# Exponentials kept in one fixed SBUF tile and summed by tensor_reduce, with row sums a stretch later and more work on GpSimd

## The chip, the core and the metric

The kernel runs on one core of one Trainium2 chip. The core has TensorE (matrix products into PSUM), VectorE, ScalarE, GpSimd, and SyncE (SP), which here issues nearly all DMAs. The metric is the device time of one execution in microseconds (us). Before the change it is 2807.87 us, the median of 3 runs (2807.44 to 2809.33).

## What is computed

Two attention blocks over images of 512 channels and 32 x 32 places; 8 images, all float32. Cut to what matters:

```python
def L0(x):                                  # 8 heads of 64 channels
    h = group_norm(x, groups=32)
    q, k, v = split(einsum('oc,bct->bot', w_qkv, h) + b_qkv)
    weight = softmax(einsum('bct,bcs->bts', q * scale, k * scale), axis=-1)
    a = einsum('bts,bcs->bct', weight, v)
    return x + einsum('oc,bct->bot', w_proj, a) + b_proj

def L1(x):                                  # one head of 512 channels
    xn = group_norm(x, groups=8)
    q, k, v = conv1x1(xn, q_w, q_b), conv1x1(xn, k_w, k_b), conv1x1(xn, v_w, v_b)
    attn = softmax(einsum('bqc,bck->bqk', q, k) / sqrt(512), axis=-1)
    return x + conv1x1(einsum('bqk,bkc->bqc', attn, v), p_w, p_b)

x = L1(L0(x))
```

A softmax is computed without subtracting the maximum: exponentials, their product with the values, and a division by the sums of the exponentials afterwards.

## The kernel before

**Products.** Large products use a seven-product (Winograd) form of the 2 x 2 block product; convolutions of layer 0 use it twice, one inside the other. Each needs sums and differences of its operands ("factors"): `left_sums`, `right_sums`, `image_factors` (t, and differences in place), `inner_factors` (four differences of 128 x 256 for each of the seven products, made in the order 1, 5, 2, 6, 7, 3, 4), `query_factors`. TensorE's instructions are all pinned to the order in which the program writes them; others are pinned only where the text says `keep_in_program_order`, and otherwise ordered by a scheduler by readiness and program order.

**Layer 0's attention** (`attention0`, one call per image) goes over 4 pairs of heads (hp) and 2 halves of the queries (tb): 8 *stretches*. In a stretch, 8 times (s): two products give scores into a PSUM tile `sc` [128, 2, 512] (three such tiles, six banks), and ScalarE takes the exponential into a tile `e` of 128 x 1024 (L658). VectorE adds the eight tiles up, one add after another, into `total` (L660, L662). Then the products of values and exponentials go into `av`. ScalarE copies `av` to `a` (L681). After the second half of a head pair `scale` (L694) calls `reciprocals`: products with a column of ones add the totals over the partitions ("row sums"), VectorE copies the result to a line (L617), and a chain of DMAs on SP turns it into columns, takes it back after VectorE's reciprocal, and spreads it over the partitions as `r`. One stretch of products later VectorE multiplies `a` by `r` (L696), and SP stores it to `kept`. For the last head pair GpSimd multiplies, and the row sums come behind the first product of the next stage. In the last image (`store` is None) the output is not kept, and the order differs.

**Hooks.** Other work is put into the 8 stretches by a list `extra` of 16 hooks: number 2n is run after the scores of stretch n, number 2n + 1 after its values. In images 1 to 6 they carry the residual adds (0), group-norm statistics (1, 3), the group mean (4), its scale (5), the normalisation on ScalarE (7, 9), and the factors of the next products (9 to 15); in image 0 the factors of a weight product z (`later`), whose DMA `prepare_z<-product_z` is issued shortly before, and the first weight loads.

**Layer 1's scores** (`scores1`) go into eight tiles `e`; ScalarE takes the exponentials in place (L739), GpSimd adds them up (L743), and VectorE (four) and GpSimd (four) take the differences that the next product needs (L786). `values1` multiplies with the values; `layer1_rest` puts these together.

**Memory.** A pool `big` has 34 buffers of 4 KB per partition, shared by images, factors, exponentials and totals, each freed after its last use. PSUM has eight banks: in layer 0's attention six hold scores, and a pool `ps_acc` of two (L185) holds, in turn, `av`, row sums, and the small products for the group mean and variance (`acc_tile`, L193).

Of the kernel before, what the change touches and what calls it, by code (L numbers as in the profile page):

```python
# [15 lines left out]
P = 128  # L16
EPS = 1e-5
ORDER = (1, 5, 2, 6, 7, 3, 4)
NBIG = 34
# [10 lines left out]
def two_attention_blocks_kernel(  # L30
# [143 lines left out]
    def main_path(ctx):  # L174
        big = ctx.enter_context(tc.tile_pool(name="big", bufs=NBIG))
        wpool = ctx.enter_context(tc.tile_pool(name="wpool", bufs=3))
# [117 lines left out]
        def keep(n, t):  # L294
            nc.sync.dma_start(wdram[n], t)
# [54 lines left out]
        def image_factors(h, uid, sub=nc.vector.tensor_sub):  # L350

            tiles = [pair_tile(f"t{i}_{uid}") for i in (1, 2, 4)]
# [57 lines left out]
        def inner_factors(hf, uid, pin=lambda ins: ins, engine=nc.gpsimd):  # L410

            f, steps = {}, []
            for p in ORDER:
                t = big_tile(f"inner{p}_{uid}", (P, 4, 2 * P))
# [178 lines left out]
        def reciprocals(totals, uid, across, direct=None):  # L593
# [17 lines left out]
            queue = direct or nc.sync  # L611
            lines = lambda d: d.rearrange("t j i n -> i (t j) n"), line[0:P:32].rearrange("p t a b -> p (t a) b")
            if direct:
                nc.vector.reciprocal(line, sums)
                queue.dma_start(lines[0](rows), lines[1])
            else:
                nc.vector.tensor_copy(line, sums)  # L617
                raw_rows = rowpool.tile([n, 2, 4, P], F32, tag=f"rows{n}", name=f"rows_{uid}")
                queue.dma_start(lines[0](raw_rows), lines[1])
                cols = small.tile([P, 16], F32, tag="cols", name=f"cols_{uid}")[:, : n * 8]  # L620
                flat = lambda t: t.rearrange("t j i n -> (t j i n)").rearrange("(p m) -> p m", p=P)
                queue.dma_start(cols, flat(raw_rows))
                recs = small.tile([P, 16], F32, tag="recs", name=f"recs_{uid}")[:, : n * 8]
                nc.vector.reciprocal(recs, cols)
                queue.dma_start(flat(rows), recs)
            if across:
                r = pair_tile(f"r_{uid}")
                for j in range(2):
                    row = rows[0, j : j + 1].rearrange("j i n -> j (i n)")
                    queue.dma_start(r[:, j, :], row.to_broadcast([P, HT]))  # L630
            else:
                r = rpool.tile([P, 2, HT], F32, tag="r", bufs=1, name=f"r_{uid}")[:, :n]
                for j in range(2):
                    row = rows[:, j : j + 1].rearrange("t o i n -> o t (i n)")
                    queue.dma_start(r[ts(j, 64)], row.to_broadcast([64, n, HT]))
            return r


        def attention0(b, q, k, v, a, extra, store=None):
            n = 0  # L640
            scaled, totals, behind = [], [], []

            for hp in range(KC):
                for tb in (0, 1) if hp < KC - 1 or store else (1, 0):
                    uid = f"0_{b}_{hp}_{tb}"
                    total = pair_tile(f"sum_{uid}")
                    es = []
                    for s in range(NS):
# [8 lines left out]
                        e = pair_tile(f"e_{uid}_{s}")  # L657
                        nc.scalar.activation(e, sc, AF.Exp, scale=(C // 8) ** -0.5)  # L658
                        if s == 1:
                            nc.vector.tensor_add(total, es[0], e)  # L660
                        elif s > 1:
                            nc.vector.tensor_add(total, total, e)  # L662
                        es.append(e)
# [10 lines left out]
                    if not (store and hp == KC - 1):  # L674
                        after, scaled = [*scaled, *after], []
                    elif tb == 1:
                        after, scaled = [*after, *scaled], []
# [23 lines left out]
                    if store and hp == KC - 1:  # L701
                        behind.append(scale)
                    else:
                        scale()

            assert not extra
# [3 lines left out]
        def scores1(f, gf, gsteps, first, uid, stats):  # L710
# [6 lines left out]
            e = {(c, cc, r): pair_tile(f"e_{uid}_{c}{cc}{r}") for r in range(2) for c in range(2) for cc in range(2)}  # L717
            total = pair_tile(f"sum_{uid}")
            parts = [pair_tile(f"sum{r}_{uid}") for r in range(2)]
# [17 lines left out]
            def exps(r, c):  # L737
# [3 lines left out]
            def add_up(r, c):  # L741

                on = lambda dst, x, y: lambda: tc.keep_in_program_order(nc.gpsimd.tensor_tensor(dst, x, y, ALU.add))  # L743
                if r == c:
                    return [on(parts[r], e[c, 0, r], e[c, 1, r])]
                return [
                    *(on(parts[r], parts[r], e[c, cc, r]) for cc in range(2)),
                    on(total[:, r, :], parts[r][:, 0, :], parts[r][:, 1, :]),
                ]

            def product(s, p, y, x, before, small, after7=(), final=()):
# [19 lines left out]
            product(1, 2, (0, 0), (1, 0), [5], gsteps[2:4], (), [lambda: exps(0, 0)])  # L771
# [3 lines left out]
            product(5, 3, (0, 1), (0, 1), [], stats[7:10] + add_up(0, 0), [lambda: exps(1, 1)], [lambda: exps(0, 1)])  # L775
            product(
                6, 4, (1, 0), (1, 0), [], stats[10:] + add_up(1, 1) + add_up(0, 1), (),
                [lambda: exps(1, 0), lambda: background.extend(add_up(1, 0) + steps)],
# [3 lines left out]
            engines = [nc.vector] * 4 + [nc.gpsimd] * 4  # L782
# [3 lines left out]
                lambda *a: engines.pop(0).tensor_tensor(*a, ALU.subtract),  # L786
# [24 lines left out]
        def raw(n, i):  # L811
            ts_ = [pair_tile(f"raw{n}_{h}") for h in range(2)]
# [15 lines left out]
        def natural(wt, nm, banks):  # L828
            ts_ = [pair_tile(f"nat{nm}_{h}") for h in range(2)]
# [41 lines left out]
        def prologue():  # L871
            ident.append(big_tile("ident", (P, P)))
            make_identity(nc, ident[0])
            raw_k = raw("k", 5)
            raw_q = raw("q", 4)
            h0 = [load_x(0, c, "h0") for c in range(KC)]
            first = {n: prepare(n) for n in "vqk"}
            wk = natural(raw_k, "k", ("a", "b"))
            wq = natural(raw_q, "q", ("c", "acc"))
# [13 lines left out]
            raw_v = raw("v", 6)  # L893
            raw_p = raw("p", 7)
# [21 lines left out]
            wv = natural(raw_v, "v", "bc")  # L916
            norm1.group_mean(acc_tile("gmean_0_1")[:, :KC])
            for f in p0_steps:
# [9 lines left out]
                1: steps, 2: [lambda: keep("z", t), load, load], 5: [load],  # L928
                12: [
# [177 lines left out]
        for b in range(B):  # L1107
# [16 lines left out]
            hf, t = image_factors(h, uid, here)  # L1124
            inner, ih = inner_factors(hf, uid, tc.keep_in_program_order)
            V = nc.vector
# [30 lines left out]
            for f in ih[4:]:  # L1157
                f()
# [21 lines left out]
            def factors_of_a():  # L1180
                af, t = image_factors(again, f"a_{b}")
                f, ia = inner_factors(af, f"a_{b}", tc.keep_in_program_order)
# [220 lines left out]
```

## Time and profile before

| | |
|---|---|
| median of 3 runs | 2807.87 us |
| the profiled execution | 2808.09 us |
| its span (first to last instruction) | 2806.3 us |
| TensorE clock granted, mean | 0.998 |
| one layer-0 stretch on TensorE | 7.07 (scores) + 7.02 (values) us |
| one image in the steady part (900.74 to 1242.63) | 341.89 us: TensorE busy 341.75, VectorE 245.83, ScalarE 124.28, GpSimd 161.92 |
| bytes moved by DMA | 320.10 MB, 114 GB/s in the mean |

Times in a profile line are microseconds; in a group of instructions the columns are line, engine, operation, output<-inputs with their shapes, count, then busy time in us and the mean of one in ns, and last the idle time of the engine just before them with what ended it. A wait is written as "engine, tile <- releaser: us in total, times, longest". In the chain that ended last, each step is followed back to what released it; its columns are start, length, and what ran. L60 is the helper that issues all matmuls, so these are told apart by tile names: `sc` scores, `av` values, `sums` row sums.

### The profile page before, as it was taken

The numbers are of one execution on the slowest core, as the hardware profiler recorded it, in microseconds if no ns is written. First come the engines' busy times: TensorE is split into PE (matmuls) and PEld (weight loads), VectorE is DVE, ScalarE is ACT, GpSimd is POOL, SyncE is SP. The second block draws the span as 40 slices with busy tenths as digits, with TensorE's granted clock in tenths as the row PEclk, the third lists the DMA queues.
The fourth block names the chain that finished last, engine by engine and source line by source line (L and its number), as shares of the span: only waits on it lengthen the run. The fifth ranks groups of instructions, "written<-read, shape, count | busy, mean of one in ns | idle before, by whom it ended". The sixth has DMA issues, their size and how long they took to land.

```text
span 2806.3 us, 35081 instructions
## 1 busy us (share of the span) xinstructions
PE 2786.6 (99%) x12756; PEld 1749.4 (62%) x12756; DVE 1981.4 (71%) x3018; ACT 986.3 (35%) x1275; POOL 1265.5 (45%) x1300
## 2 busy tenths in 40 slices
PE   9999999999999999999999999999999999999999
PEld 5436736776376853768538594485844868348584
DVE  5477777667776777766776767766678756787665
ACT  1253354214632146312463125531255212633130
POOL 2302705745067440774308652185521846137572
PEclk9999999999999999999999999999999999999999
DMA  8744512234123441134401343114521035112301
GB/s 285 226 161 139 196 32 70 111 146 178 34 67 131 152 153 39 62 139 165 148 24 62 150 174 127 32 54 161 187 102 49 37 151 207 63 55 94 120 5 73
DMA packets 118525, 320.10 MB, mean 114 GB/s; under 512 B 19591, under 2 KB 57927, under 8 KB 107722
## 3 DMA queue, kind: packets, MB, share of 16 engines
q1 hardware_dynamic: 117758, 317.36, 31.7%
q8 instruction: 103, 1.69, 0.2%
q14 instruction: 76, 0.62, 0.1%
q10 hardware_dynamic: 588, 0.42, 0.0%
HBM read 247.13 MB, written 70.62 MB: 113 GB/s over the span
## 4 chain that ended last, share of the span: by engine, by line
PE 97%; DVE 2%; issue 1%; POOL 1%; DMA 0%; ACT 0%; SPq 0%; DVEq 0%; POOLq 0%
PE sc L60 16%; PE av L60 15%; PE psb_av L60 6%; PE psb L60 5%; PE psa_av L60 4%; PE psc_av L60 4%; PE psc L60 3%; PE psa L60 3%; PE psb_z L60 3%; PE psb_g L60 3%; PE psb_k L60 3%; PE psb_q L60 3%; PE psb_v L60 3%; PE psb_p L60 2%; PE psa_z L60 2%; PE psc_z L60 2%
## 5 line engine op out<-in xcount | busy, mean ns | idle before, releaser
L658 ACT ACTIVATE e<-sc 128x1024 f32<-128x1024 f32 x512 | 476.2, 1051 | 79.7 <-PE sc L60 79.7
L662 DVE TENSOR_TENSOR sum<-sum,e 128x1024 f32<-128x1024 f32 x384 | 470.5, 1225 | 35.8 <-ACT x L138 0.5
L60 PE MATMUL sc<-q,k 64*128 64x512 f32 x2048 | 458.4, 597 | 0.0
L60 PE MATMUL av<-e,v 128*64 128x512 f32 x2048 | 453.4, 595 | 0.0
L60 PEld LDWEIGHTS sc<-q,k 64*128 64x128 f32 x2048 | 190.7, 186 | 247.3 <-ACT e L658 120.3
L60 PEld LDWEIGHTS av<-e,v 128*64 128x64 f32 x2048 | 141.4, 137 | 299.0 <-issue 289.0
L421 POOL TENSOR_TENSOR inner_h<-x 128x256 f32<-128x256 f32 x16 | 14.8, 924 | 415.8 <-DVE x L1105 415.8
L660 DVE TENSOR_TENSOR sum<-e,e 128x1024 f32<-128x1024 f32 x64 | 79.2, 1237 | 103.7 <-ACT e L658 103.7
L681 ACT COPY a<-av 128x512 f32<-128x512 f32 x64 | 37.6, 587 | 319.4 <-PE av L60 308.1
L126 POOL TENSOR_TENSOR rstd<-ve,mhalf 128x4 f32<-128x4 f32 x16 | 16.7, 1043 | 263.9 <-DVE ve L124 263.9
L60 PE MATMUL psb<-inner,inner_h 128*128 128x256 f32 x448 | 115.6, 380 | 0.0
L60 PE MATMUL psa_av<-e,z 128*128 128x512 f32 x256 | 113.3, 595 | 0.0
L421 POOL TENSOR_TENSOR inner_h<-h 128x256 f32<-128x256 f32 x30 | 24.1, 805 | 186.9 <-DVE h L1105 119.8
L743 POOL TENSOR_TENSOR sum<-sum,e 128x1024 f32<-128x1024 f32 x32 | 81.4, 2543 | 28.9 <-ACT e L739 27.7
L60 PEld LDWEIGHTS psb<-inner,inner_h 128*128 128x128 f32 x448 | 84.5, 190 | 13.6 <-POOL inner L436 1.8
L469 ACT COPY psb_v<-psa_v 128x512 f32<-128x512 f32 (+1 forms) x28 | 14.5, 517 | 218.9 <-DVE x L805 155.1
L60 PE MATMUL psb_g<-inner_h,w_m 128*128 128x256 f32 x336 | 86.5, 385 | 0.3
L729 DVE TENSOR_TENSOR e<-psc,u 128x512 f32<-128x512 f32 x56 | 38.7, 691 | 65.5 <-PE psc L60 65.3
L542 POOL TENSOR_TENSOR v<-v,v 128x256 f32<-128x256 f32 x28 | 20.1, 727 | 143.5 <-DVE u_v L537 143.4
L60 PEld LDWEIGHTS psa_av<-e,z 128*128 128x128 f32 x256 | 48.0, 190 | 57.3 <-issue 56.6
L421 POOL TENSOR_TENSOR inner_h<-t_h 128x256 f32<-128x256 f32 x62 | 73.3, 1187 | 21.3 <-PE psc_av L60 16.1
L739 ACT ACTIVATE e<-e 128x1024 f32<-128x1024 f32 x64 | 65.3, 1053 | 46.7 <-DVE e L729 25.6
(433 smaller groups left out, 6088.6 us busy)
## 6 DMA issues: line engine op xcount, KB each, us to landing
r<-all_rows SPq DMA_DIRECT2D x78, 256.0 KB
x<-in_x SPq DMA_DIRECT2D x36, 512.0 KB
h<-in_x SPq DMA_DIRECT2D x32, 512.0 KB
spill<-x SPq DMA_DIRECT2D x32, 512.0 KB
x<-spill SPq DMA_DIRECT2D x32, 512.0 KB
out<-x SPq DMA_DIRECT2D x64, 256.0 KB
kept<-a SPq DMA_DIRECT2D x28, 512.0 KB
again<-kept SPq DMA_DIRECT2D x28, 512.0 KB
```

The costliest lines, as they stand in the source:

```text
L60: tc.keep_in_program_order(nc.tensor.matmul(*args, **kw))
L126: nc.gpsimd.tensor_tensor(rstd, ve, mhalf, ALU.pow)
L421: pin(engine.tensor_tensor(dst, x, y, ALU.subtract))
L469: nc.scalar.copy(ps["b"], ps["a"])
L542: nc.gpsimd.tensor_tensor(d, x, y, ALU.add)
L658: nc.scalar.activation(e, sc, AF.Exp, scale=(C // 8) ** -0.5)
L660: nc.vector.tensor_add(total, es[0], e)
L662: nc.vector.tensor_add(total, total, e)
L681: nc.scalar.copy(dst, av)
L729: nc.vector.tensor_add(dst[0], ps, x[0])
L739: nc.scalar.activation(e[c, cc, r], e[c, cc, r], AF.Exp, scale=scale)
L743: on = lambda dst, x, y: lambda: tc.keep_in_program_order(nc.gpsimd.tensor_tensor(dst, x, y, ALU.add))
```

## The change

- The eight exponentials of a layer-0 stretch go to fixed places of one tile `exps` of nine places of 4 KB (0 to 3 and 5 to 8). In images 0 to 6 VectorE adds places 0 to 3 into place 4 by one `tensor_reduce` after the fourth exponential, and places 4 to 8 into the total by a second after the eighth. Neighbours within a reduction are one place, 4 KB, apart. The last image keeps the adds.
- The row sums of the first three head pairs come one stretch later, after the scores; their copy to a line moves to ScalarE; the scaling comes after the values of the stretch after that, on GpSimd.
- In these images the differences of `image_factors` and all of `inner_factors` move from VectorE to GpSimd.
- In layer 1 VectorE sums the exponentials by eight `tensor_reduce` of 128 columns each, and GpSimd takes all eight differences.
- `big` has 26 buffers; raw and transposed weights of the start, the attention output that is read back (`again`) and some of its factors use places of `exps`.
- In image 0 the hooks of z's factors and of the weight loads move later.

```diff
-NBIG = 34
+NBIG = 26
...
+        epool = ctx.enter_context(tc.tile_pool(name="epool", bufs=1))
+        exps = epool.tile([P, 9, 2, HT], F32, tag="exps", name="exps")
...
-                nc.vector.tensor_copy(line, sums)
+                copy(line, sums)
...
+            sums, due = [], {}
+            after_sc, whole = exps[:, 4], lambda lo, hi: exps[:, lo:hi].rearrange("p s j n -> p (j n) s")
...
+                    flat = total.rearrange("p j n -> p (j n)")
+                    stretch = n // NS
+                    es = [exps[:, s + s // 4] for s in range(NS)]
+                    for s, e in enumerate(es):
...
                         nc.scalar.activation(e, sc, AF.Exp, scale=(C // 8) ** -0.5)
-                        if s == 1:
+                        if store:
+                            if s == 3:
+                                nc.vector.tensor_reduce(after_sc.rearrange("p j n -> p (j n)"), whole(0, 4), AX.X, ALU.add)
+                            elif s == NS - 1:
+                                nc.vector.tensor_reduce(flat, whole(4, 9), AX.X, ALU.add)
+                        elif s == 1:
                             nc.vector.tensor_add(total, es[0], e)
...
-                    for f in extra.pop(0) if extra else ():
+                    for f in [*sums, *(extra.pop(0) if extra else ())]:
                         f()
+                    sums = []
                     av = acc_tile(f"av_{uid}")
...
+                    if store:
+                        after = [*after, *due.pop(stretch, ())]
...
-                    engine = nc.gpsimd if hp == KC - 1 and not direct else nc.vector
+                    engine = nc.gpsimd if store or hp == KC - 1 and not direct else nc.vector
...
-                        r = reciprocals(totals, uid, False, nc.scalar if direct else None)
+                        copy = nc.scalar.copy if store and hp < KC - 1 else nc.vector.tensor_copy
+                        r = reciprocals(totals, uid, False, nc.scalar if direct else None, copy)
...
+                    elif hp < KC - 1:
+                        sums.append(scale)
+                        due[stretch + 2] = scaled
...
-            e = {(c, cc, r): pair_tile(f"e_{uid}_{c}{cc}{r}") for r in range(2) for c in range(2) for cc in range(2)}
+            e = {(c, cc, r): exps[:, 5 * r + 2 * c + cc] for r in range(2) for c in range(2) for cc in range(2)}
...
+            def add_up(r):
+
+                every = exps[:, 5 * r : 5 * r + 4].rearrange("p s i n -> p n (s i)")
                 return [
+                    lambda n=n: tc.keep_in_program_order(
+                        nc.vector.tensor_reduce(total[:, r, ts(n, P)], every[:, ts(n, P), :], AX.X, ALU.add)
+                    ) for n in range(HT // P)
                 ]
...
-            engines = [nc.vector] * 4 + [nc.gpsimd] * 4
...
-                lambda *a: engines.pop(0).tensor_tensor(*a, ALU.subtract),
+                lambda *a: tc.keep_in_program_order(nc.gpsimd.tensor_tensor(*a, ALU.subtract)),
...
-                1: steps, 2: [lambda: keep("z", t), load, load], 5: [load],
-                12: [
+                3: steps, 4: [lambda: tc.keep_in_program_order(keep("z", t)), load], 8: [load], 12: [
+                    load,
...
-            hf, t = image_factors(h, uid, here)
+            hf, t = image_factors(h, uid, here if last else on_pool)
...
-                    9: [*t[:2], lambda: ih[0](V)], 11: [*t[2:4], lambda: ih[1](V), lambda: ih[3](V)],
-                    13: [lambda: ih[2](V)], 15: t[4:],
+                    9: [*t[:2], ih[0]], 11: [*t[2:4], ih[1], ih[3]], 13: [ih[2], *t[4:6], ih[4]], 15: [*t[6:], ih[5]],
...
-                again[c] = big_tile(f"again_{b}_{c}")
-                nc.sync.dma_start(again[c], kept[c])
+                again[c] = exps[:, c].rearrange("p j n -> p (j n)")
+                tc.keep_in_program_order(nc.sync.dma_start(again[c], kept[c]))
```

More of the change, by code (lines that the diff above doesn't have):

```diff
@@ L347, in weight, with image_factors @@
             return weight_factors(weight_part(n))
-        def image_factors(h, uid, sub=nc.vector.tensor_sub):
-            tiles = [pair_tile(f"t{i}_{uid}") for i in (1, 2, 4)]
+        def image_factors(h, uid, sub=nc.vector.tensor_sub, slots=()):
+            tiles = [exps[:, i] for i in slots] or [pair_tile(f"t{i}_{uid}") for i in (1, 2, 4)]
             halves = lambda t: (t[:, :HT], t[:, HT:])
@@ L590, in conv2, with reciprocals @@
             return out
-        def reciprocals(totals, uid, across, direct=None):
+        def reciprocals(totals, uid, across, direct=None, copy=nc.vector.tensor_copy):
             n = len(totals)
@@ L673, in attention0 @@
                     after = extra.pop(0) if extra else []
-                    if not (store and hp == KC - 1):
+                    if store:
+                        after = [*after, *due.pop(stretch, ())]
+                    else:
                         after, scaled = [*scaled, *after], []
-                    elif tb == 1:
-                        after, scaled = [*after, *scaled], []
                     for f in after:
@@ L700, in attention0 @@
                     totals = []
-                    if store and hp == KC - 1:
+                    if not store:
+                        scale()
+                    elif hp < KC - 1:
+                        sums.append(scale)
+                        due[stretch + 2] = scaled
+                    else:
                         behind.append(scale)
-                    else:
-                        scale()
-            assert not extra
+            assert not extra and not sums and not due
             return scaled, behind
@@ L735, in more, with exponentials @@
                 )
-            def exps(r, c):
+            def exponentials(r, c):
                 for cc in (1, 0):
                     nc.scalar.activation(e[c, cc, r], e[c, cc, r], AF.Exp, scale=scale)
[L741 to L745, printed above, removed]
+            def add_up(r):
+                every = exps[:, 5 * r : 5 * r + 4].rearrange("p s i n -> p n (s i)")
                 return [
-                    *(on(parts[r], parts[r], e[c, cc, r]) for cc in range(2)),
-                    on(total[:, r, :], parts[r][:, 0, :], parts[r][:, 1, :]),
+                    lambda n=n: tc.keep_in_program_order(
+                        nc.vector.tensor_reduce(total[:, r, ts(n, P)], every[:, ts(n, P), :], AX.X, ALU.add)
+                    ) for n in range(HT // P)
                 ]
@@ L808, in values1, with raw @@
             wino(f"av_{uid}", mm, done, middle=(2, 5, 6, 7), hooks=hooks, back=4)
-        def raw(n, i):
-            ts_ = [pair_tile(f"raw{n}_{h}") for h in range(2)]
+        def raw(n, i, slot=None):
+            ts_ = [pair_tile(f"raw{n}_{h}") if slot is None else exps[:, slot + h] for h in range(2)]
             for kc in range(KC):
@@ L826, in main_path, with natural @@
         ident = []
-        def natural(wt, nm, banks):
-            ts_ = [pair_tile(f"nat{nm}_{h}") for h in range(2)]
+        def natural(wt, nm, banks, slot):
+            ts_ = [exps[:, slot + h] for h in range(2)]
             t = [ts_[o // 2][:, o % 2, :] for o in range(KC)]
@@ L892, in prologue @@
             )
-            raw_v = raw("v", 6)
-            raw_p = raw("p", 7)
+            raw_v = raw("v", 6, 0)
+            raw_p = raw("p", 7, 2)
             for f in first["v"][1]:
@@ L1156, in main_path @@
             scaled, behind = attention0(b, q, k, v, a, extra, lambda hp: nc.sync.dma_start(kept[hp], a[hp]))
-            for f in ih[4:]:
-                f()
+            ih[6]()
             psum_pools(f"products_{b}", 2)
```

42 lines of the change are left out of this document (20 added, 22 removed).

## The prediction

> **What bounds the kernel now.** I read the page's first part, then TensorE's own waits, then the chain that ended last, and only then single engines. Busy time and waits:
>
> ```profile
> PE 2786.6 (99%) x12756; PEld 1749.4 (62%) x12756; DVE 1981.4 (71%) x3018; ACT 986.3 (35%) x1275; POOL 1265.5 (45%) x1300
> ...
> PE sums L60 <- DVE sum L662: 5.1, 1, 5.1
> PE tr_wk L63 <- DMA rawk<-in_w: 3.6, 1, 3.6
> PE psa_v L60 <- POOL h L140: 0.8, 1, 0.8
> ```
>
> The first line is engine by engine, the others are all of TensorE's waits above 0.5 us (total, times, longest). TensorE is busy for 2786.6 of 2806.3 us; it waits for VectorE once for long. The other 60 or so stretches have no wait at all, so nothing that only lightens VectorE or GpSimd can be seen in the end time. The one wait, in the chain that ended last (start, length, what):
>
> ```profile
> 133.46 1.94 PE sc L60 x8
> ...
> 136.29 5.02 DMA prepare_z<-product_z
> ...
> 141.38 0.70 DVE prepare_z L289
> ...
> 144.01 1.15 DVE sum L660
> ...
> 153.17 1.08 PE sums L60 x8
> 154.25 8.63 PE sc L60 x32
> 162.89 7.02 PE av L60 x32
> 169.90 7.07 PE sc L60 x32
> ```
>
> In image 0's second stretch VectorE stands behind a weight transfer that lands at 141.3, so its eight-tile sum is late, and TensorE waits in the middle of the row sums. The scores after it take 8.63 us instead of 7.07; over 147.5 to 162.9 the profile shows a granted clock of 0.78. The stall costs 154.18 - (147.48 + 1.00) = 5.70 us (row sums started at 147.48 and last 1.00 elsewhere), plus 8.63 - 7.07 = 1.56: **7.3 us**.
>
> **The added reduction.** In images 0 to 6 each stretch (scores 7.07, values 7.02, so 14.09 us of TensorE) gets two tensor_reduces over strided places: 1024 x 4 = 4096 and 1024 x 5 = 5120 elements per partition. They replace seven adds. The rows nearest:
>
> ```profile
> L1213 DVE TENSOR_REDUCE extreme<-every_row x2: 744/744/744, 2763.0 to 2763.7; 128x1 f32<-128x576 f32 x2
> ...
> L662 DVE TENSOR_TENSOR sum<-sum,e 128x1024 f32<-128x1024 f32 x384 | 470.5, 1225 | 35.8 <-ACT x L138 0.5 <-DVE sum L662 0.5 <-ACT e L658 0.5
> L786 DVE TENSOR_TENSOR t<-e,e 128x1024 f32<-128x1024 f32 x16 | 36.0, 2289 | 0.0
> L1105 DVE TENSOR_TENSOR x<-x,x 128x512 f32<-128x512 f32 x14 | 9.0, 685 | 0.0
> ```
>
> From 1225 ns for 1024 and 685 ns for 512 a VectorE element costs 1.055 ns and an instruction 145 ns; the only reduction of before, contiguous, fits that: (744 - 145)/576 = 1.04 ns. Lower bound: 1.04 ns, so 4.41 + 5.47 = 9.9 us a stretch against 7 x 1.225 = 8.6. The upper bound must come from far: a stream held up by its operands is L786, 2289/1024 = 2.24 ns, so 20.9 us a stretch. No row has a stride of 4 KB between neighbours. I take the lower end, because L1213 is the same operation with one source and few results, while L786 is two sources with GpSimd working on the same tiles at once.
>
> The Trainium skill disagrees in part: "Vector Engine (DVE) Microarchitecture Reference", section "Measured stream behaviour on trn2", has 1.73 ns per column where one of two sources hops 4 KiB at every element, but full rate for a one-source op that alternates between two regions and writes one word per two reads. No row here shows either; ours resembles the second; by 1.73 VectorE would end image by image behind TensorE and the time would be about 2957 (estimate, by the sum in the first rival). "SBUF — State Buffer", section "Who interferes with whom", speaks for the change: tensor_reduce doesn't hold GpSimd off, two-input VectorE operations do; L786's 2289 beside L662's 1225 agrees.
>
> **Does VectorE stay hidden?** An attention stage is 8 x 14.09 + 3 x 1.00 (row sums) + 0.3 = 116.0 us (331.63 to 447.6 in image 1). VectorE's other work left in it: 8 bn_stats at 0.675, 4 aggregates at 0.204, five small ones near 0.16 and three reciprocals at 0.25, 7.8 us. With 8 x 9.9 that is 87 of 116. Moved away are 24 subtractions (8 x 0.69 + 16 x 0.42 = 12.2), three scalings (3 x 1.37) and three copies (3 x 0.69). So VectorE is no fuller than before (88.1 busy between 331.6 and 446.0). Within a stretch: exponential 4 of 8 ends about 1.2 + 4 x 0.93 = 4.9 us after the scores start, the first reduction ends at 9.3, the second at 14.8; the next exponential into its places is due at 14.1 + 4.9 = 19.0, the first half's at 15.3. Nothing waits. If this cover is gone, at (116 - 7.8 - 16 x 0.145)/73,728 = 1.44 ns an element, VectorE sets the pace.
>
> **The row sums.** The total is complete 0.7 us after the stretch, so sums at its end would stall; moved behind the next scores they don't. Image 0's stall goes too: its weight sums are queued a stretch later, behind a reduction that ends near 148.3, when the 141.3 landing is past. That is **-7.3 us**. On SP, image 0's write of the z sums and its three weight loads move from hooks 2, 2, 2, 5 to 4, 4, 8, 12; the last, 1.8 MB, starts near 214 and takes 7 us at the 276 GB/s moved from 147.5 to 162.9, for a use at 264: 0. What is late next: the PSUM tiles. Values, row sums and both group-norm products share two acc banks (L185, L193). In the third stretch of images 1 to 6, row sums and group mean now both stand between scores and values; values need one bank back. The row-sum copy is on ScalarE, behind the eighth exponential:
>
> ```profile
> 345.83 0.59 ACT L681 COPY a<-av 128x512 f32<-128x512 f32 x1 [5.54 <-PE av L60]
> 346.89 7.44 ACT L658 ACTIVATE e<-sc 128x1024 f32<-128x1024 f32 x8 [0.47 <-PE sc L60]
> ```
>
> Columns: start, length, operation. These scores started at 345.71, so the exponentials end 8.6 us after the start; a copy of 0.59 beginning as they drain ends near 9.1. TensorE is ready at 7.07 + 1.00 + 0.14 = 8.2. Wait 0.9 us, six times: **+5.4 us**. Bounds: 0, if the copy were earlier, and 8.6 - 8.2 + 0.69 + 0.1 = 1.2 us a time. The other two row sums of an image find a bank free. Their DMAs on SP (line, columns, reciprocals back, two broadcasts, then the store) have a stretch and a half, 21 us, against 4 serial steps of 2 to 2.6 us; the GpSimd scaling that waits for them has other GpSimd work ahead of it that is ready.
>
> **GpSimd.** Attention gains 8 subtractions of 512 (1.27 us, row L734) and 16 of 256 (0.73), 21.8 us, and three scalings at 2.35: 29 us onto 10.8 busy of 116. Before the next products the last factors end near 110. In layer 1 it loses six sums (18.2 us an image, L743) and gains four differences of 2.35 (9.4): from 518.8 the eight differences take 18.8, to 537.6; the first is used at 551.8, and the scaling behind them still ends at 540, as now. VectorE's eight small reductions there (1024 elements, 1.2 us each) fit between evictions; the second half ends near 525.6 and is needed at 530.5. All hidden: 0.
>
> **Buffers.** 34 shared tiles become 26 and nine fixed places; stages that held eight exponentials keep their margin. In the value convolution the places stand idle while eight tiles fewer rotate: GpSimd's factors end there at 577 and are needed from 587. Cover 10 us; I take 0, bounds 0 and 3 us an image. Raw weights in fixed places load after their transposes (7.3 us), are used from 100: 0.
>
> **Sum.** The profiled execution is 2808.1 us around a span of 2806.3, beside a median of 2807.9 (2807.4 to 2809.3). 2808.1 - 7.3 + 5.4 = 2806.2; against the median, **2806.0**.
>
> **Rivals.** *The strided reduction is dear* (slower; chance 0.30). From 1.44 ns on, the exponentials wait for places that VectorE still reads. An image then takes 73,728 x p + 10.1 us in attention: at 2.24 ns 175.3, 59.3 too much, seven times, so 2806 + 415 = 3221; at 1.8 ns 25.8 x 7, so about 2987. For it: no row shows such a stride. Against: L1213's slope and a single source. *No bank wait* (faster; 0.24): ScalarE's copy lies ahead of the last exponential, or the mean elsewhere; the stall's gain stays whole, 2807.9 - 7.3 = 2800.6. Against it: eight exponentials were queued first. *New small waits* (slower; 0.14): factors or loads late for want of buffers, 1 to 3 us in each of seven images on top, 2813 to 2827. For it: GpSimd is full from 557 to 577. *The forecast* has 0.32.
>
> **How the numbers follow.** A measurement here tells 0.2%, 5.6 us, from no change: 2802.3 to 2813.5. The forecast lies inside (its own range 2802 to 2812), so same 0.32; faster 0.24 from the second rival; slower 0.30 + 0.14 = 0.44. The range begins at 2797, the second rival with 3 us to spare, and ends at 3000, where the price is 1.81 ns ((116 + 27.7 - 10.1)/73,728): above it lies about half of the first rival, 0.14.
>
> **What would show it.** Reductions of 4.4 and 5.5 us and no wait of TensorE at 148 to 153 show the first steps right; 7 to 9 us and scores waiting for exponentials in every stretch show the first rival. Six waits of values for a row-sum copy, about 0.9 us each, show the bank step; none, the second rival. Waits in products for factors show the third. A wholly different wait, or a clock below 0.99 in steady images, would make the prediction wrong.

## The result, and the profile after

| | before | changed |
|---|---|---|
| median | 2807.65 us | 3075.09 us |
| range of the runs | 2807.44 to 2809.33 | 3074.23 to 3075.76 |
| profiled span | 2806.3 us | 3073.8 us |

The changed kernel takes 1.0951 times as long, with a 95% interval of 1.0932 to 1.0970: it is slower by 267 us. The forecast was 2806.0 and its range ended at 3000.

First come the busy times of the whole page, then TensorE's own waits (what waited, for what: total us, times, longest us).

```profile
PE 2874.4 (94%) x12756; PEld 1770.6 (58%) x12756; DVE 2344.4 (76%) x2560; ACT 1002.6 (33%) x1296; POOL 1358.5 (44%) x1457
```

```profile
PE sc L60 <- ACT exps L665: 85.3, 34, 5.2
PE sums L60 <- DVE sum L670: 40.2, 7, 6.0
PE gvar L60 <- DVE dv L119: 36.4, 7, 6.1
PE psb L60 <- DVE exps L744: 8.9, 7, 1.3
PE psb_q L60 <- DVE u_q L542: 5.4, 7, 0.8
PE av L60 <- ACT line L622: 5.0, 6, 0.9
PE tr_wk L63 <- DMA exps<-in_w: 3.8, 1, 3.8
PE psb_z L60 <- DVE exps L744: 3.4, 8, 2.3
```

TensorE issues as many matmuls as before (12756), but the share of time in which it is busy falls from 99% to 94%. The 267 us have two parts. The waits that the profile lists come to 192 us instead of 12, so about 180 us more; and the same matmuls are busy for 2874.4 us instead of 2786.6, 88 us more, at a mean granted clock of 0.970 instead of 0.998. The 5.1 us for the row sums of image 0 is off the list. In its place stand 34 waits of scores for exponentials, seven waits for row sums and seven for the group variance, most of them near 6 us. All three end at VectorE. For the exponentials that is read one engine further, from the groups of instructions of ScalarE (busy us, mean ns of one | idle before, what ended it): half of their own idle time ends with a reduction, which must leave a place before it is written again.

```profile
L665 ACT ACTIVATE exps<-sc 128x1024 f32<-128x1024 f32 x512 | 482.9, 1034 | 202.5 <-PE sc L60 100.8 <-DVE sum L670 81.2 <-DVE exps L668 19.9
```

The reductions, in the same columns:

```profile
L670 DVE TENSOR_REDUCE sum<-exps 128x1024 f32<-128x5120 f32 x56 | 507.3, 9059 | 6.1 <-DVE exps L668 0.5
L668 DVE TENSOR_REDUCE exps<-exps 128x1024 f32<-128x4096 f32 x56 | 411.9, 7355 | 49.4 <-ACT exps L665 47.0
...
L761 DVE TENSOR_REDUCE sum<-exps 128x128 f32<-128x1024 f32 x64 | 120.6, 1927 | 0.0
```

Per element that is 7355/4096 = 1.80 ns and 9059/5120 = 1.77 ns, where the forecast took 1.04. The two reductions of a stretch need 16.4 us; TensorE's scores and values need 14.09. The chain that ended last says the same: before, 97% of it was TensorE's, now a quarter is VectorE's, of which L670 has 12% of the span and L668 10%. First before, then after:

```profile
PE 97%; DVE 2%; issue 1%; POOL 1%; DMA 0%; ACT 0%; SPq 0%; DVEq 0%; POOLq 0%
```

```profile
PE 59%; DVE 25%; ACT 2%; POOL 1%; issue 1%; DMA 0%; DVEq 0%; ACTq 0%; POOLq 0%
```

How one stall breeds another is seen in image 1. VectorE, in order of time (start, length, operation, idle before it and what ended that):

```profile
396.13 7.36 DVE L668 TENSOR_REDUCE exps<-exps 128x1024 f32<-128x4096 f32 x1 [0.27 <-ACT exps L665]
403.59 8.93 DVE L670 TENSOR_REDUCE sum<-exps 128x1024 f32<-128x5120 f32 x1
...
413.13 0.16 DVE L119 TENSOR_TENSOR dv<-d,mv 128x4 f32<-128x4 f32 x1
...
421.68 7.45 DVE L668 TENSOR_REDUCE exps<-exps 128x1024 f32<-128x4096 f32 x1 [7.66 <-ACT exps L665]
429.23 9.07 DVE L670 TENSOR_REDUCE sum<-exps 128x1024 f32<-128x5120 f32 x1
```

and TensorE over the same time:

```profile
400.30 7.09 PE L60 MATMUL av<-exps,v 128*64 128x512 f32 x32 [0.79 <-ACT line L622]
413.44 0.38 PE L60 MATMUL gvar<-dv,gm 128*64 128x4 f32 x4 [6.06 <-DVE dv L119]
413.75 10.20 PE L60 MATMUL sc<-q,k 64*128 64x512 f32 x32
```

The group mean's chain of four small VectorE instructions (the last of them is L119) stands behind a reduction of 8.93 us. TensorE, in order, waits for it for 6.06 us, the scores behind it start late and run slowly (10.20 us instead of 7.07), and so VectorE, now the engine that sets the pace, has nothing to reduce for 7.66 us. The windows over image 1's attention give the sum, with columns of time, busy us of TensorE, weight loads, VectorE, ScalarE and GpSimd (instructions), granted clock, DMA share, GB/s. Before:

```profile
331.63:447.60 115.97, 115.97 (x570) 43.18 (x570) 89.72 (x107) 68.10 (x75) 11.77 (x9) 1.00 0.18 58
```

After:

```profile
352.32:506.29 153.97, 130.87 (x590) 47.00 (x589) 138.67 (x39) 71.76 (x80) 47.32 (x47) 0.90 0.14 47
```

VectorE is busy for 138.67 of 153.97 us, TensorE's clock drops to 0.90, and the stage takes 38 us more.

### The profile page after: what moved, and what is told of

The parts are those of the page before. It is cut to its first block, busy times and chain, and to the rows that moved or that the text cites. A ratio compares the mean times of both kernels' runs of the same rounds, so it can differ in the third digit from the quotient of the medians.

```text
span 3073.8 us, 34683 instructions
## 1 busy us (share of the span) xinstructions
PE 2874.4 (94%) x12756; PEld 1770.6 (58%) x12756; DVE 2344.4 (76%) x2560; ACT 1002.6 (33%) x1296; POOL 1358.5 (44%) x1457
## 4 chain that ended last, share of the span: by engine, by line
PE 59%; DVE 25%; ACT 2%; POOL 1%; issue 1%; DMA 0%; DVEq 0%; ACTq 0%; POOLq 0%
DVE sum L670 12%; DVE exps L668 10%; PE psb_av L60 5%; PE psb L60 5%; PE psa_av L60 4%; PE psc_av L60 4%; PE psc L60 3%; PE av L60 3%; PE sc L60 3%; PE psa L60 3%; PE psb_g L60 3%; PE psb_z L60 2%; PE psb_v L60 2%; PE psb_k L60 2%; PE psb_p L60 2%; PE psa_z L60 2%
## 5 line engine op out<-in xcount | busy, mean ns | idle before, releaser
L60 PE MATMUL sc<-q,k 64*128 64x512 f32 x2048 | 497.1, 631 | 85.3 <-ACT exps L665 85.3
L665 ACT ACTIVATE exps<-sc 128x1024 f32<-128x1024 f32 x512 | 482.9, 1034 | 202.5 <-PE sc L60 100.8
L670 DVE TENSOR_REDUCE sum<-exps 128x1024 f32<-128x5120 f32 x56 | 507.3, 9059 | 6.1 <-DVE exps L668 0.5
L60 PE MATMUL av<-exps,v 128*64 128x512 f32 x2048 | 466.9, 609 | 5.0 <-ACT line L622 5.0
L668 DVE TENSOR_REDUCE exps<-exps 128x1024 f32<-128x4096 f32 x56 | 411.9, 7355 | 49.4 <-ACT exps L665 47.0
L60 PEld LDWEIGHTS av<-exps,v 128*64 128x64 f32 x2048 | 144.2, 141 | 318.0 <-issue 308.6
L709 POOL TENSOR_TENSOR a<-a,r 128x1024 f32<-128x1024 f32 (+1 forms) x29 | 67.5, 2328 | 335.7 <-DMA r<-all_rows 335.7
L761 DVE TENSOR_REDUCE sum<-exps 128x128 f32<-128x1024 f32 x64 | 120.6, 1927 | 0.0
L60 PE MATMUL psa_av<-exps,z 128*128 128x512 f32 x256 | 113.3, 596 | 0.0
L60 PE MATMUL sums<-sum,ones 128*32 128x256 f32 x576 | 51.6, 471 | 40.3 <-DVE sum L670 40.2
L754 ACT ACTIVATE exps<-exps 128x1024 f32<-128x1024 f32 x64 | 65.0, 1051 | 71.0 <-DVE exps L744 49.9
```

What stands on the lines that cost most here:

```text
L60: tc.keep_in_program_order(nc.tensor.matmul(*args, **kw))
L668: nc.vector.tensor_reduce(after_sc.rearrange("p j n -> p (j n)"), whole(0, 4), AX.X, ALU.add)
L670: nc.vector.tensor_reduce(flat, whole(4, 9), AX.X, ALU.add)
L709: scaled.append(lambda: tc.keep_in_program_order(engine.tensor_tensor(dst, dst, r, ALU.mult)))
L761: nc.vector.tensor_reduce(total[:, r, ts(n, P)], every[:, ts(n, P), :], AX.X, ALU.add)
```

## The experiments

Three theories stood at the start. S: the strided walk over the places is what costs, and nothing else of the change costs much. R and B, its rivals: any reduction of this length costs so much, or the places collide in a memory bank because they lie a round 4 KB apart. A second question followed: what does the change cost when the reductions are cheap?

**The reduction by itself.** Both attention blocks are left out; VectorE and GpSimd run the disputed operations on one loaded tile. Shortened, the two views are:

```
hop  = lambda k, step: src[:, : k * step].rearrange("p (k m) -> p m k", k=k)[:, :1024, :]
near = lambda k: src[:, : k * 1024].rearrange("p (m k) -> p m k", k=k)
nc.vector.tensor_reduce(one[:, :1024], hop(4, 1024), AX.X, ALU.add)   # places 4 KB apart
nc.vector.tensor_reduce(one[:, :1024], near(4), AX.X, ALU.add)        # neighbours
```

> Only a row of VectorE and GpSimd operations on one tile, each four times; both attention blocks are left out. Theory S (the hop between neighbours costs): a reduction of 4096 elements takes 7.2 to 7.5 us with neighbours 4 KB apart, 4.4 us with neighbours adjacent; 5120: 9.0 against 5.5; two places (2048 elements) 3.7 against 2.3; eight places 14.6 against 8.7; 1024 elements 2 KB apart 1.9 against 1.2. Theory R (a result every few elements costs, not the hop): adjacent takes as long as apart, and 4096 elements into one result take 4.4 us. Theory B (the same bank is hit again and again): with places 4 KB + 32 bytes apart it falls to 4.4 us; by S it stays near 7.3. Last part: if reductions leave GpSimd alone, its six adds of 1024 beside them take 2.35 us each, and more (3 us or above) beside VectorE adds.

Measured, in ns for one reduction, with 1024 results except in the last row (128 results):

| places | spread | adjacent |
|---|---|---|
| 2 | 2297 | 2297 |
| 4 | 7085 | 4420 |
| 5 | 8792 | 5486 |
| 8 | 13911 | 8686 |
| 4, with 32 bytes between places | 7085 | |
| 8, 2 KB apart, 128 results | 1872 | 1220 |

A reduction of 4096 elements into one result also took 4420 ns. The four-place rows of the two views as the trace groups them, first spread and then adjacent:

```profile
L57 DVE TENSOR_REDUCE one<-src 128x1024 f32<-128x4096 f32 x4 | 28.3, 7085 | 6.1 <-DMA src<-in_x 6.0
```

```profile
L57 DVE TENSOR_REDUCE one<-src 128x1024 f32<-128x4096 f32 x4 | 17.7, 4420 | 0.1
```

Then four places with 32 bytes between them, and the eight reductions over two places, four spread and four adjacent:

```profile
L57 DVE TENSOR_REDUCE one<-src 128x1024 f32<-128x4096 f32 x4 | 28.3, 7085 | 0.1
```

```profile
L57 DVE TENSOR_REDUCE one<-src 128x1024 f32<-128x2048 f32 x8 | 18.4, 2297 | 0.3
```

The same instruction with the same shapes takes 1.60 times as long when neighbours of the sum lie in different places. From 4 to 8 places an element costs (13911 - 7085)/4096 = 1.67 ns, against (8686 - 4420)/4096 = 1.04. R falls, since adjacent elements cost what the forecast assumed; B, as it was put, falls, since shifting the places by 32 bytes changes nothing; larger shifts were not tried. One expectation of S missed: two places alternate at full rate (2297 ns, not about 3700). So the cost of the walk is shown, but not why four places cost it and two do not, nor at which distance between neighbours it begins.

The four-place figure, 7085/4096 = 1.73 ns, is what "Vector Engine (DVE) Microarchitecture Reference" of the Trainium skill, section "Measured stream behaviour on trn2", gives for one of two sources hopping 4 KiB. Its other statement, full rate for one source alternating between two regions, agrees with our two places (2297/2048 = 1.12 with the instruction's fixed part). The prediction applied that statement about two regions to four and five places, and these do not run at full rate.

**The changed kernel with adjacent elements.** The totals are other sums; instructions, sizes and places are those of the change.

```
-after_sc, whole = exps[:, 4], lambda lo, hi: exps[:, lo:hi].rearrange("p s j n -> p (j n) s")
+after_sc, whole = exps[:, 4], lambda lo, hi: exps[:, lo:hi].rearrange("p s j n -> p (s j n)").rearrange("p (m s) -> p m s", s=hi - lo)
...
-every = exps[:, 5 * r : 5 * r + 4].rearrange("p s i n -> p n (s i)")
+every = lambda n: exps[:, 5 * r + n].rearrange("p i m -> p (i m)").rearrange("p (m k) -> p m k", k=8)
```

> The changed kernel with the same number of reductions, elements and results, but each result sums 4, 5 or 8 adjacent elements, so the row totals are other sums than the reference's. Theory S: VectorE takes 4.4 and 5.5 us again and leaves the path; what is left is the prediction's sum, 2807.6 - 7.3 + 5.0 (the six bank waits as measured) = 2805, between 2800 and 2812. Theory R: 3075, as with the change. Theory O (something else of the change: fewer buffers, GpSimd's scaling waiting for DMA, the copy on ScalarE): 2850 or more.

2829.33 us, ratio to the kernel before 1.0074 (1.0058 to 1.0091), with reductions of 4414 and 5486 ns. The stride is 3075.1 - 2829.3 = 245.8 us of the loss. But the time is above the 2800 to 2812 expected, by about 20 us, and TensorE's waits say where:

```profile
PE sc L60 <- ACT exps L665: 9.3, 6, 1.6
PE psb_q L60 <- DVE u_q L542: 5.5, 7, 0.9
PE av L60 <- ACT line L622: 4.8, 6, 0.8
PE tr_wk L63 <- DMA exps<-in_w: 4.3, 2, 3.9
PE gvar L60 <- DVE dv L119: 3.8, 1, 3.8
```

The largest, the scores, is read from VectorE in image 1's first two stretches:

```profile
336.42 0.64 DVE L91 BATCH_NORM_STATS2 bnst<-x 128x6 f32<-128x512 f32 x1
...
337.22 4.37 DVE L668 TENSOR_REDUCE exps<-exps 128x1024 f32<-128x4096 f32 x1
341.68 5.49 DVE L670 TENSOR_REDUCE sum<-exps 128x1024 f32<-128x5120 f32 x1
347.26 4.42 DVE L668 TENSOR_REDUCE exps<-exps 128x1024 f32<-128x4096 f32 x1
```

The statistics of all four channels stand ahead of the first reduction, though their hooks lie behind it. The second reduction ends at 347.2, and only then may the next stretch's exponentials write the places that it reads: scores wait 1.6 us.

**The changed kernel with additions in layer 0.** Seven adds a stretch in place of two reductions; layer 1 keeps its strided ones.

```
-if store:
-    if s == 3:
...
-elif s == 1:
+if s == 1:
     nc.vector.tensor_add(total, es[0], e)
```

> The changed kernel with seven adds a stretch in place of the two reductions in layer 0; all else as changed, the eight strided reductions of layer 1 too. Theory S: layer 0 is hidden again; layer 1 keeps reductions of 1.9 us, with some 2 us of TensorE waits an image: 2807.6 - 7.3 + 5.0 + 8 x 2 = 2821, between 2808 and 2830. Theory O: 2900 or more.

2836.70 us, ratio 1.0102 (1.0085 to 1.0119), slightly above the expectation. The 85 us of waiting scores are gone; left are products of layer 1 behind the small reductions (8.9 and 3.4 us), the query products (5.4), the bank (4.8) and seven short waits for the row sums (3.0). So the layer-0 reductions carry most of the loss, and the rest of the change is not free.

**The group mean later.** In the changed kernel the mean goes to hook 5, the scale to 7, the first normalisations to 8.

```
-3: [*stats[2:], store], 4: [mean],
-5: [affine], 7: applies[:2], 9: applies[2:],
+3: [*stats[2:], store], 5: [mean],
+7: [affine], 8: applies[:2], 9: applies[2:],
```

> The changed kernel with the group mean one hook later, its scale two hooks later and the first normalisations one hook later. Theory S with a chain (TensorE waits 6 us for the group mean's small operations behind the second reduction, and VectorE then idles 7.7 us for the next exponentials): six images lose that, 3075 - 6 x 7 = 3033, between 3025 and 3045. If VectorE's throughput alone counts and that idle time is made up elsewhere: 3070 to 3076.

3035.73 us, ratio 1.0805 (1.0787 to 1.0823). This is 39.4 us below the changed kernel, 6.6 in each of six images: the stall at 413 us above, with what it bred, was worth that much. Of the seven waits for the variance one of 2.1 us is left, and the six for the bank are gone, 39.3 us of waiting together. It is a net figure: scores now wait more often for exponentials (44 times and 97.6 us instead of 34 and 85.3), and TensorE's busy time is 11.5 us shorter (2862.9).

**The kernel before with image 0's later hooks alone.** The sums of the z weights and the weight loads move together, as in the change.

```
-1: steps, 2: [lambda: keep("z", t), load, load], 5: [load],
-12: [
+3: steps, 4: [lambda: tc.keep_in_program_order(keep("z", t)), load], 8: [load], 12: [
+    load,
```

> The kernel before with one part of the change alone: image 0's sums of the z weights and the weight loads of its first stretches go to the later hooks; nothing else differs. Theory S (the prediction's step: VectorE no longer stands behind the transfer of the z products when the second stretch's eighth addition is due): TensorE's wait of 5.1 us for the row sums at 148 to 153 us is gone and the scores after it take 7.1 us instead of 8.6, so 2807.9 - 7.3 = 2800.6 us (2799.5 to 2802.5). Rival R (the wait only goes to the next row sums, or to the z products' own users): within 3 us of the kernel before, with a new wait of 4 us or more in image 0. A third way, if the weight loads come too late for the first products: slower than 2808.

2800.36 us (2799.82 to 2801.24), ratio 0.9972 (0.9961 to 0.9982): 7.3 us below the 2807.65 of the result, and 7.7 below the 18 runs of the kernel before that were taken beside it (2808.01), as the term of the prediction says. The chain that ended last, over image 0's second and third stretch:

```profile
141.46 7.02 PE av L60 x32
148.48 1.00 PE sums L60 x16
149.48 7.07 PE sc L60 x32
```

The row sums, 16 matmuls, run without a break. This version beats both kernels, and it has none of the reductions.

**The 21 us that the stride does not explain.** Three versions start from the one with adjacent elements. The first keeps the statistics at their hooks:

```
-norm = GroupNorm(1, f"1_{b}", halves=True)
+norm = GroupNorm(1, f"1_{b}", pinned=True, halves=True)
```

> The version with the adjacent reductions (its totals are other sums), 2829.3 us, with one edit: the group-norm statistics of the projection's output keep their place at hooks 1 and 3, so they stand behind the first stretch's two reductions on VectorE's queue instead of ahead of the first. Theory L (what is left of the loss, 21 us, is the sum of single waits that the profile lists): the six waits of scores for exponentials (9.3 us in total, 1.6 each) are gone and the time is 2829.3 - 9.3 = 2820.0, with the scores slowed after a wait perhaps 2818 (2817 to 2822). Rival D (the rest is a general slowing, by places, loads or contention, and the listed waits are only where it comes to light): the wait goes to another stretch or another tile, and the time stays above 2825.

2818.92 us, ratio 1.0039 (1.0025 to 1.0053): 10.4 us less, and the six waits of scores are gone. The second lets the differences of the loaded attention output move again:

```
-af, t = image_factors(again, f"a_{b}", here, slots=(5, 6, 7))
+af, t = image_factors(again, f"a_{b}", slots=(5, 6, 7))
```

> The version with the adjacent reductions (its totals are other sums) with one edit: the differences of the attention output that is loaded again (made on VectorE in the query convolution) are no longer tied to their places in the queue, as in the kernel before. Theory L: the seven waits of the query products for their evictions (5.5 us, 0.8 each) are gone, 2829.3 - 5.5 = 2823.8 (2822 to 2825). Rival D: no change, 2828 to 2830.5, because the differences take 0.98 us instead of 0.69 beside GpSimd's work on the same tile wherever they stand.

2826.22 us, ratio 1.0065 (1.0051 to 1.0079): 3.1 us less, where 5.5 was expected. The seven waits shrank to one of 0.3, but 1.0 us of others came up in the key products. The third has both edits and the later group mean:

> The version with the adjacent reductions (its totals are other sums) with both of these edits, and the group mean a hook later (hook 5, the scale at hook 7, the first normalisations at hook 8), so that values find a free bank in the third stretch. Theory L: gone are the waits of scores (9.3), of query products (5.5), of values for the row-sum copy (4.8) and of the group variance (3.8): 2829.3 - 23.4 = 2805.9; with the 2 to 3 us by which the products after such waits run slower, 2803 (2801 to 2808). That is the kernel before less image 0's 7.3 us, plus at most 5. Rival D: above 2815.

2808.47 us, ratio 1.0003 (0.9994 to 1.0012). It is 20.9 us below where it started, half a microsecond past the end of theory L's range; the variance's 3.8 us, which it counted as gone, stayed. The remainder was for the most part a sum of single waits, and over 900 to 1250 us TensorE is as busy as before (349.86 of 350). It is still 8.1 us behind the version with the later loads alone, and the largest part is one wait in the last image:

```profile
PE gvar L60 <- DVE dv L119: 3.8, 1, 3.8
```

VectorE and GpSimd at that place:

```profile
2591.18 3.46 DVE L761 TENSOR_REDUCE sum<-exps 128x128 f32<-128x1024 f32 x3
2594.56 0.15 DVE L113 COPY gmean<-gmean 128x4 f32<-128x4 f32 x1
2594.75 1.97 DVE L115 TENSOR_TENSOR d<-mv,gmean 128x4 f32<-128x4 f32 x1
2596.75 2.27 DVE L117 TENSOR_TENSOR d<-d 128x4 f32<-128x4 f32 x1
2599.05 2.26 DVE L119 TENSOR_TENSOR dv<-d,mv 128x4 f32<-128x4 f32 x1
```

```profile
2594.35 4.65 POOL L799 TENSOR_TENSOR t<-exps,t 128x1024 f32<-128x1024 f32 x2
2598.95 2.33 POOL L799 TENSOR_TENSOR exps<-exps 128x1024 f32<-128x1024 f32 x1
```

Operations on four columns, 0.16 us elsewhere, take about 2 us each, and each ends as one of GpSimd's differences ends (2594.35 + 2.33 = 2596.7; 2599.0; 2601.3). But the mean's product was ready at 2590.6 and VectorE only came to it at 2594.56, behind the reductions of layer 1. Two causes are possible, so the next run took GpSimd's four added differences away there.

**Half of the differences on VectorE again in the last such stage.**

```
+engines = [nc.vector] * 4 + [nc.gpsimd] * 4
...
-lambda *a: tc.keep_in_program_order(nc.gpsimd.tensor_tensor(*a, ALU.subtract)),
+lambda *a: engines.pop(0).tensor_tensor(*a, ALU.subtract)
+if stats else tc.keep_in_program_order(nc.gpsimd.tensor_tensor(*a, ALU.subtract)),
```

> The three-edit version (2808.5 us; its totals are other sums) with one edit in the last of layer 1's stages that runs beside a group norm: the first four of the eight differences of exponentials are on VectorE and untied, as before, in place of eight tied ones on GpSimd. In the three-edit version three VectorE operations of four columns take 1.97, 2.27 and 2.26 us there, each ending when a GpSimd difference ends, and TensorE waits 3.8 us for the group variance; the products after it run slower. Theory P (a two-input VectorE operation, however small, takes turns with GpSimd's): at most one such long one is left, the wait is below 1 us, and the time is 2808.5 - 3.8 - 1.7 = 2803.0 (2802 to 2805). Rival Q (VectorE's own queue of strided and other reductions makes the variance late): the wait stays between 3 and 5 us, 2808 to 2810.

2810.42 us, ratio 1.0009 (1.0000 to 1.0018): not faster, and the wait grew to 5.1 us. This does not settle it. Two long operations were left (2.33 and 2.30 us), not one at most, and VectorE's own differences came between the steps of the mean; in both versions three reductions lie ahead. The split between VectorE's queue and its turns with GpSimd stays open; it concerns under 6 us of 267. In the three-edit version the two seem to be needed together: TensorE came for the variance at 2597.6, and with operations of 0.16 us the chain would have ended near 2595.3 in spite of the queue (an estimate from the rows above). The next run has a longer queue there (three reductions in 5.68 us instead of 3.46) but only one long operation (2.29 us), and TensorE waits 2.1 us instead of 3.8.

**Layer 1's strided reductions alone.** The three-edit version with the changed kernel's view in layer 1:

```
-every = lambda n: exps[:, 5 * r + n].rearrange("p i m -> p (i m)").rearrange("p (m k) -> p m k", k=8)
+every = exps[:, 5 * r : 5 * r + 4].rearrange("p s i n -> p n (s i)")
```

> The three-edit version (2808.5 us; its layer-0 totals are other sums) with the layer-1 sums back as the change has them: eight reductions an image of 1024 elements, neighbours 2 KB apart, 1.9 us each in the changed kernel instead of 1.2. Theory S (a strided reduction in front of an eviction on VectorE is paid in full, as the changed kernel's waits of the products for VectorE in layer 1 say: 8.9 and 3.4 us in total): 2808.5 + 12.3 = 2820.8 (2818 to 2823). Rival H (the prediction's step: they fit between evictions, and the waits of the changed kernel come from its delayed images): 2808 to 2811.

2824.40 us, ratio 1.0058 (1.0044 to 1.0071): 15.9 us more than with adjacent elements. The waits are exactly those of the changed kernel:

```profile
PE psb L60 <- DVE exps L744: 8.9, 7, 1.3
...
PE psb_z L60 <- DVE exps L744: 3.4, 8, 2.3
```

So they do not come from delayed images. The time is 3.6 us above the 12.3 that these waits explain. The profile has the rest: TensorE's busy time is 5.2 us longer (2792.9 against 2787.7), and the wait for the variance is 1.7 us shorter.

**The ledger**, each step a difference of medians, read in this order (another order would share them out differently):

| step | us |
|---|---|
| kernel before | 2807.65 |
| later z sums and weight loads (image 0's stall gone) | -7.3 |
| change with adjacent elements and three repairs, against that | +8.1 |
| the three repairs undone: statistics 10.4 alone, query differences 3.1 alone, group mean the remaining 7.4 | +20.9 |
| the stride, in both layers, with the stalls that it breeds | +245.8 |
| changed kernel | 3075.1 |

The later row sums, their copy on ScalarE, GpSimd's added work and the smaller pool were not tried one by one; together they stand in the +8.1, beside the 3.8 us of the variance.

## Why the prediction was wrong

**The step that failed** is the price of the added reduction: "I take the lower end, because L1213 is the same operation with one source and few results". L1213 reads contiguous elements. With the bounds named there, 1.04 and 2.24 ns, the truth was 1.77 to 1.80, past the prediction's own break-even of 1.44. The argument from one source was no argument: the run of the reduction alone has one source, no GpSimd beside it, and 1.73 ns. The 0.27 us by which the kernel's reductions are longer than those alone (7355 against 7085 ns) are explained in part: beside GpSimd's adds two such reductions took 7202 ns each. The upper bound came from a row of another kind. Two-input adds of 1024 on VectorE took 1224 ns alone and 3072 beside GpSimd's adds, and L786's mean of 2289 mixes durations from 1211 to 3371 ns: it measures GpSimd working at the same time, not a walk over places. That the truth lay between the two bounds was luck.

**The first rival was the right mechanism**, at 0.30, and its own sum was too small: at 1.8 ns it gave about 2987, and 3075 was measured. (By its own formula the 25.8 us an image should be 26.8, and the time 2994.) It counted VectorE's work alone. Not in it were the start of the stage (in image 1 the first reduction starts 10.8 us into it: four exponentials are there after about 5 us, but the group-norm statistics stand ahead), the last reduction that the row sums then wait for (40.2 us over seven images), the group-mean chain behind a long reduction (39.4 us with the bank waits, measured), and layer 1's eight small reductions (15.9 us, measured). Nor was the slower clock, 0.90 in that stage. These overlap and do not add up.

**Image 0's stall: right.** 7.3 us predicted, 7.3 to 7.7 measured alone.

**The bank wait: right.** Six waits of values for the row-sum copy, 5.0 us in total, against 5.4 predicted; with the mean a hook later they are gone. What they alone cost in the end time was not measured.

**"All hidden: 0" for GpSimd and layer 1, and no wait within a stretch: wrong in small sizes.** The step "the first reduction ends at 9.3, the second at 14.8 ... Nothing waits" left out that statistics without a fixed place go ahead of the first reduction and push both: 10.4 us. "VectorE's eight small reductions there (1.2 us each) fit between evictions" holds at 1.2 us and not at 1.9: 15.9 us. The differences tied to their places in the query convolution delay an eviction: 3.1 us. Small new waits, as the third rival has them, were thus there too, underneath the first, but not for its reason: they come from the order of work on VectorE, not from a want of buffers. With adjacent elements the change measured 2829, just above that rival's 2813 to 2827.

**Loads and buffers: nothing against them.** The later weight loads cost nothing that shows. Apart from the raw weights of the start, which TensorE waits for before as after (3.8 and 4.5 us), no wait in the changed kernel's list is for a transfer.

## What to carry to other kernels

Price a reduction by its walk, not by its size: count over how many separate regions one sum goes, and where the profile has no row with that walk, measure one instruction before trusting the nearest row. Once an engine holds instructions of 9 us, look for every short chain that must pass through its queue between two matmuls; here moving a group mean of four small instructions was worth 39 us. And test what a bundled change contains piece by piece: the one part that was tried alone, image 0's z sums and loads at later hooks, is a gain of 0.28% without the rest.

## What was not expected of the hardware

- Two regions alternate at full rate (2297 ns for 2048 elements, spread or adjacent), four do not (7085 against 4420), and 32 bytes between the places make no difference.
- Two-input adds pay for the distance of elements too: with every second word of both inputs 1223 ns for 1024, as for contiguous inputs (1224); with every fourth word 1964.
- GpSimd's adds took 2351 ns each beside VectorE's reductions and 3057 beside its two-input adds, which themselves took 3072 instead of 1224; the rows of GpSimd, beside the one and then the other:

```profile
L94 POOL TENSOR_TENSOR gx<-gx 128x1024 f32<-128x1024 f32 x6 | 14.1, 2351 | 0.4
...
L100 POOL TENSOR_TENSOR gx<-gx 128x1024 f32<-128x1024 f32 x6 | 18.3, 3057 | 0.4
```

- A wait can cost more than its length: scores after a 6.06 us wait took 10.20 us instead of 7.07, and the granted clock over them was 0.70. Not every wait does: after the same wait of 3.61 us in image 1, the values took 8.70 us in the changed kernel and 7.09 with the group mean later. What decides it was not followed.
